# A hybrid graph-attention and Mamba network on one core: x of the first batch loaded first and in pieces, its group norm ahead of the mixer's weights, decay rates and taps broadcast by their loads

## The chip, the core and the metric

The kernel runs on one core of a Trainium2 chip, as a single launch. The core has five engines that each work through a queue of their own: TensorE (PE in the profile; its weight loads are listed apart, as PEld), VectorE (DVE), ScalarE (ACT), GpSimd (POOL) and SyncE (SP), which here only issues DMAs. The metric is the time of one execution on the device in microseconds, and lower is better. Several executions are timed and the median is given.

## What is computed

The network has four layers on x of shape (4 batches, 32 time steps, 128 nodes, 128 features). Only the start of layer 0 bears on this change. Layer 0 adds to x the result of a graph attention over the nodes followed by a Mamba mixer over the time steps, both on a group norm of x. Cut to that:

```python
def _gn(v, G=32, eps=1e-5):                 # per batch, over time, nodes and 4 features of a group
    g = v.reshape(B_, H_, W_, G, C_ // G)
    m = jnp.mean(g, axis=(1, 2, 4), keepdims=True)
    s = jnp.var(g, axis=(1, 2, 4), keepdims=True)
    return ((g - m) / jnp.sqrt(s + eps)).reshape(v.shape)

x = x + _L0_conv_ref(_gn(x), adj, Wq, Wk, Wv, Wo, bo, ...)
# in it: h = layernorm(h + gat(h, adj, Wq, Wk, Wv, Wo, bo)); then, per node, the mixer on h:
xz = xt @ in_proj
xc, z = xz[..., :256], xz[..., 256:]
xconv = conv_b + sum(conv_w[:, kk] * xp[:, kk:kk + T, :] for kk in range(4))   # the taps
xc = silu(xconv)
dbc = xc @ x_proj
dt = softplus(dbc[..., :8] @ dt_w + dt_b)
A = -jnp.exp(A_log)                          # (256, 16) decay rates
dA = jnp.exp(dt[..., None] * A)
h_t = dA_t * h_(t-1) + dt_t * xc_t * B_t     # scan over the 32 steps
y_t = sum over states of h_t * C_t, + Dp * xc, times silu(z), @ out_w + out_b
```

The group norm of a batch needs all 32 time steps of that batch and nothing of the other batches. The decay rates A are the same for every node, and so are the four taps per channel.

## The kernel before

x stays in SBUF for the whole program as the tile X, with nodes on the 128 partitions, then 128 (batch, time) pairs, then 128 features. The program is built in order: `open` makes constants, `load_x` loads X, `layer0` and the three further layers follow.

`load_x` (line 260) issues four DMAs from SyncE's queue, one per batch, each of 4096 rows of 512 bytes. `layer0` (line 266) then loads and prepares weights. `gat_weights` (line 289) loads six tiles of 64 KB and three columns, all from SyncE's queue, and makes `far` (a mask from the adjacency matrix) and `identb`. `mamba_weights` (line 576) loads the mixer's weights and prepares two large tables that hold the same values on all 128 partitions, because in the mixer the nodes are on the partitions and the channels along the row:

- Ar, 128 x 16 x 256, the decay rates. A_log comes as a small tile with channels on partitions; ScalarE takes its exponential, VectorE negates it, TensorE transposes it, and sixteen matmuls with a column of the identity spread one row each over the partitions, each followed by a copy out of PSUM (lines 607 to 625).
- Wm, 128 x 4 x 256, in_proj times the taps. The taps are transposed with A_log, spread by four matmuls, and multiplied in by VectorE (lines 626 to 633).

After this comes the group norm of batch 0, `gat_head` (line 311): in eight groups of four time steps TensorE transposes x into one of two PSUM banks called pm (line 257), ScalarE copies it to S (line 329) and VectorE takes statistics (line 334). Then these are aggregated (line 344), summed over the four features of a group by two tiny matmuls with g4, and eight VectorE instructions normalize S in place (line 374). The attention `gat` (line 378) begins with matmuls of S with Wq and Wk and their copies out of PSUM by ScalarE (lines 405 and 408). Its buffers lie in the pool l0g, opened after the head.

The mixer `mamba` (line 644) runs once per batch. Its `decay` multiplies dt by Ar on GpSimd (line 675), and `expo` takes the exponential on ScalarE (line 681); there are 496 of each. The group norm of batches 1 to 3 is placed at the end of the mixer of the batch before it (line 848).

The order of work around the change is set in two ways. Instructions of one engine run in the order in which they stand in its queue. The order inside `gat_head`, `gat` and `mamba` is written by a small planner, `Parts`, from costs and dependences given by hand, and pinned by `in_order` (line 227). Outside of these, the tile framework orders instructions itself; so `identb` and `I2` stand ahead of `far` in VectorE's queue. The framework also gives every DMA one of eight completion semaphores in turn; a DMA whose semaphore was used by an earlier one waits on its queue until the earlier one has landed.

Of the kernel before, what the change touches and what calls it, by code (L numbers as in the profile page):

```python
# [12 lines left out]
F32 = mybir.dt.float32  # L13
BF16 = mybir.dt.bfloat16
AF = mybir.ActivationFunctionType
ALU = mybir.AluOpType
# [3 lines left out]
P = 128  # L20
B, T, N, F = 4, 32, 128, 128
# [166 lines left out]
class Kernel:  # L188
# [68 lines left out]
            self.nc.tensor.transpose(pt[:, i, :], s, self.ident[:k, :k])  # L257


    def load_x(self):  # L260
        for b in range(B):
            self.nc.sync.dma_start(
                self.X[:, b * T : (b + 1) * T, :], self.ins["x"][b].rearrange("t n f -> n t f")
            )

    def layer0(self):

        with self.pool("l0h", 1) as hp, self.pool("l0c", 1) as c:
            h1 = hp.tile([P, 3 + T, N], F32, tag="h1", name="h1")
            self.nc.gpsimd.memset(h1[:, :3, :], 0.0)  # L270
            with self.pool("l0k", 1) as k, self.pool("l0kp", 2, True) as pk:
                gw, mw = self.gat_weights(c), self.mamba_weights(c, k, pk)


            with self.pool("l0s", 1) as m, self.pool("l0w", 2) as w, self.pool("l0pm", 2, True) as pm:
                S = m.tile([P, T * N], F32, tag="S", name="S")
                plan = Parts()
                self.gat_head(plan, 0, S, gw, m, pm)
                with self.in_order():
                    plan.emit()  # L280
                for b in range(B):
                    with self.pool("l0g", 2) as g, self.pool("l0sc", 1, True) as ps, self.pool("l0po", 1, True) as po:
                        with self.pool("l0px", 1, True) as px:
                            blk = self.gat(h1, S, gw, mw, g, m, w, ps, po, px, pm)
                    with self.pool("l0m", 1) as y, self.pool("l0m2", 2) as v:
                        with self.pool("l0pa", 2, True) as pa, self.pool("l0y", 1, True) as py:
                            self.mamba(b, h1, S, blk, gw, mw, m, w, y, v, pa, py, pm)

    def gat_weights(self, c):
        nc, ins = self.nc, self.ins  # L290
        Wq, Wk, Wv, Wo = (self.load(c, n, ins[f"L0_conv_{n}"], [P, P]) for n in ("Wq", "Wk", "Wv", "Wo"))
        g4 = self.load(c, "g4", ins["g4"], [P, P])

        adj = self.load(c, "adj", ins["L0_conv_adj"], [P, P])
        far = c.tile([P, P], BF16, tag="far", name="far")
        nc.vector.tensor_scalar(far, adj, 0.0, 1e30, ALU.is_equal, ALU.mult)
        identb = c.tile([P, P], BF16, tag="identb", name="identb")
        nc.vector.tensor_copy(identb, self.ident)
        bo = self.col(c, "bo", ins["L0_conv_bo"])
        nsg = self.col(c, "nsg", ins["L0_conv_ns_g"])  # L300
        nsb = self.col(c, "nsb", ins["L0_conv_ns_b"])
        return Wq, Wk, Wv, Wo, g4, far, identb, bo, nsg, nsb
# [270 lines left out]
            plan.emit()  # L573
        return blk

    def mamba_weights(self, c, k, pk):
# [19 lines left out]
        for j in range(2):  # L596
            nc.vector.tensor_scalar(DD[:, j, :], ident, Dp[:, j : j + 1], None, ALU.mult)
        I2 = c.tile([P, 64], F32, tag="I2", name="I2")
        nc.vector.tensor_tensor(I2, ident[:, :64], ident[:, 64:], ALU.add)
        ob4 = c.tile([1, 4, P], F32, tag="ob4", name="ob4")  # L600
        for i in range(4):
            nc.sync.dma_start(ob4[:, i, :], ins["L0_conv_out_b"].rearrange("(o n) -> o n", o=1))
        ntg = self.row(c, "ntg", ins["L0_conv_nt_g"])
        ntb = self.row(c, "ntb", ins["L0_conv_nt_b"])

        cw = self.load(k, "cw", ins["L0_conv_conv_w"].rearrange("(c p) k -> p c k", p=P), [P, 2, 4])
        A = self.load(k, "A", ins["L0_conv_A_log"].rearrange("(c p) s -> p c s", p=P), [P, 2, 16])
        nc.scalar.activation(A, A, AF.Exp)
        nc.vector.tensor_scalar(A, A, -1.0, None, ALU.mult)
        rows = k.tile([16, 2, 2, P], F32, tag="rows", name="rows")  # L610
        for j in range(2):
            p = pk.tile([P, 2, P], F32, tag="pk", name="pk")
            nc.tensor.transpose(p[:16, 0, :], A[:, j, :], ident)
            nc.tensor.transpose(p[:4, 1, :], cw[:, j, :], ident)
            nc.vector.tensor_copy(rows[:, 0, j, :], p[:16, 0, :])
            nc.vector.tensor_copy(rows[:4, 1, j, :], p[:4, 1, :])

        Ar = c.tile([P, 16, 256], F32, tag="Ar", name="Ar")
        for s in range(16):
            p = pk.tile([P, 256], F32, tag="pr", name="pr")  # L620
            nc.tensor.matmul(
                p, ident[:16, s : s + 1].to_broadcast([16, P]),
                rows[:, 0].rearrange("p j d -> p (j d)"), start=True, stop=True,
            )
            nc.scalar.copy(Ar[:, s, :], p)
        Wm = c.tile([P, 4, 256], F32, tag="Wm", name="Wm")
        for m in range(4):
            p = pk.tile([P, 256], F32, tag="pr", name="pr")
            nc.tensor.matmul(
                p, ident[:4, 3 - m : 4 - m].to_broadcast([4, P]),  # L630
                rows[:4, 1].rearrange("p j d -> p (j d)"), start=True, stop=True,
            )
            nc.vector.tensor_tensor(Wm[:, m, :], inp[:, :256], p, ALU.mult)
        return inp, xp, dtw, ow, cb, DD, I2, ob4, ntg, ntb, Ar, Wm
# [9 lines left out]
    def mamba(self, b, h1, S, blk, gw, mw, m0, w0, m, w, pa, py, pm):  # L644
# [15 lines left out]
        hF, S = S, S.rearrange("p (s d) -> p s d", s=16)  # L660
# [4 lines left out]
        def step(t, g, before):  # L665

            k, i = divmod(t, 4)
            cs, h, v, parts = slice(i * P, i * P + P), g["h"], {}, {}
# [9 lines left out]

            def expo(q):
                v["a", q] = pa.tile([P, 4, 256], F32, tag="pa", name="pa")  # L680
                nc.scalar.activation(v["a", q], v.pop(("e", q)), AF.Exp)  # L681

            def diag(q):
                v["D", q] = w.tile([P, 4, 64], F32, tag="D", name="D", bufs=4)
# [2227 lines left out]
```

## Time and profile before

| | us |
|---|---|
| three runs | 4092.22, 4085.39, 4095.92 |
| their median | 4092.22 |
| the profiled execution | 4087.14 |
| its span, first to last instruction | 4085.3 |
| its mean granted TensorE clock | 0.891 of full speed |

Where the span goes by stage, read from the busy time of the engines in stretches (layer 0 ends near 2386 us, when the first loads of layer 1 are issued):

| stretch, us | PE busy | DVE busy | ACT busy | POOL busy | granted clock |
|---|---|---|---|---|---|
| 0 to 102 | 50.67 | 31.32 | 26.67 | 10.18 | 0.95 |
| 350 to 600 (attention, then mixer) | 213.25 | 237.47 | 220.88 | 232.21 | 0.91 |
| 2390 to 2990 (layer 1) | 461.84 | 398.19 | 257.58 | 180.37 | 0.76 |
| 3520 to 4086 (layer 3) | 446.50 | 286.09 | 332.79 | 200.97 | 0.88 |

Busy time is the time in which an engine executed something. In the mixer VectorE and GpSimd are busy over 90% of the time. The first hundred microseconds are different from all the others: no engine is busy for much over half of them.

The last lines of SyncE's queue in this stretch are issues of 0.4 us each, one after the other: for instance bo at 29.05, Dp at 33.63, ntg at 35.38 and cw at 36.26. VectorE's first DD product, which needs Dp, starts at 35.82.

### The profile page before, as it was taken

The page shows a single profiled execution, that of the slowest core. Times are in us where ns is not written, and L with a number is a line of the kernel's source. Part 1 is how long each engine was busy: PE and PEld are TensorE (multiplying, and loading weights), DVE is VectorE, ACT ScalarE, POOL GpSimd, SP SyncE. Part 2 cuts the span into 40 slices and gives each one's busy share as a digit, 9 for nine tenths or more (in the row PEclk, how much of TensorE's full clock was granted, in tenths as well). Part 3 has the DMA queues.
Part 4 walks back from the last instruction along what each step waited for, and adds up shares of the span by engine and source line. Part 5 has one row for each costly group of instructions (what it writes and reads, how often), then busy time and mean ns, then how long its engine had stood idle before and what let it go on. Part 6 is the DMA issues. An engine that isn't in the chain of part 4 may idle for free. (4 is left out here: it accounts for less than half of the span.)

```text
span 4085.3 us, 64261 instructions
## 1 busy us (share of the span) xinstructions
PE 3284.1 (80%) x23384; PEld 2080.5 (51%) x23384; DVE 3077.7 (75%) x7597; ACT 2647.8 (65%) x5230; POOL 2332.0 (57%) x1691
## 2 busy tenths in 40 slices
PE   4888887888887888878888878887747878888777
PEld 2444544445544445444444556654436634466545
DVE  3889997799997799987899964678758763545842
ACT  2699884699875799856898833345545562366753
POOL 0399993599873799963899830424444431114840
PEclk9999899999888899988999776888779999798989
DMA  2000000000000000000000000000020005100002
GB/s 93 1 1 1 1 1 1 1 1 1 1 1 1 1 1 1 1 1 1 1 1 1 1 18 1 1 1 1 1 91 1 1 1 191 64 1 1 1 0 83
DMA packets 48684, 58.74 MB, mean 14 GB/s; under 512 B 6207, under 2 KB 27404, under 8 KB 48364
## 3 DMA queue, kind: packets, MB, share of 16 engines
q1 hardware_dynamic: 34636, 39.91, 2.9%
q10 hardware_dynamic: 13728, 14.68, 1.0%
q8 instruction: 187, 3.06, 0.3%
q14 instruction: 133, 1.09, 0.1%
HBM read 46.19 MB, written 8.39 MB: 13 GB/s over the span
## 5 line engine op out<-in xcount | busy, mean ns | idle before, releaser
L675 POOL TENSOR_TENSOR e<-dt,Ar 128x1024 f32<-128x1024 f32 x496 | 1161.9, 2366 | 102.4 <-ACT pa L681 100.2
L703 DVE SCALAR_TENSOR_TENSOR S<-u,BC,pa 128x256 f32<-128x256 f32 x1984 | 820.8, 476 | 28.4 <-PE yp L718 0.5
L695 DVE TENSOR_TENSOR pa<-pa,S 128x1024 f32<-128x1024 f32 x496 | 607.4, 1225 | 51.7 <-ACT pa L681 51.4
L681 ACT ACTIVATE pa<-e 128x1024 f32<-128x1024 f32 x496 | 504.7, 1022 | 123.6 <-DVE S L703 107.9
L718 PE MATMUL yp<-S,D 64*64 64x256 f32 x4096 | 380.1, 415 | 100.8 <-DVE S L703 84.2
L718 PE MATMUL yp<-S,Dp 64*64 64x256 f32 x4096 | 341.2, 449 | 51.0 <-DVE S L703 40.2
L718 PEld LDWEIGHTS yp<-S,D 64*64 64x64 f32 x4096 | 186.2, 140 | 265.3 <-DVE S L703 156.6
L718 PEld LDWEIGHTS yp<-S,Dp 64*64 64x64 f32 x4096 | 174.8, 152 | 204.0 <-issue 120.5
L459 POOL TENSOR_TENSOR e<-e,den 128x512 f32<-128x512 f32 x128 | 132.4, 1045 | 242.3 <-DVE den L455 180.7
L687 ACT ACTIVATE D<-I,BC 128x64 f32<-128x64 f32 x1024 | 260.8, 334 | 0.6 <-PE yp L718 0.6
L897 PE MATMUL pm<-h,Wm 128*128 128x512 f32 x512 | 242.5, 609 | 1.2 <-ACT h L519 1.2
L736 PE MATMUL pm<-I,y 128*128 128x64 f32 x1024 | 164.6, 288 | 92.6 <-ACT y L726 92.6
L447 ACT ACTIVATE e<-sc,mn 128x128 f32<-128x128 f32 x512 | 143.9, 391 | 94.9 <-DVE mn L442 93.5
L736 PEld LDWEIGHTS pm<-I,y 128*128 128x128 f32 x1024 | 151.7, 213 | 104.8 <-ACT y L726 104.8
L681 ACT ACT_TABLE_LOAD x144 | 184.8, 1283 | 20.4 <-DVE S L703 18.2
L692 POOL TENSOR_TENSOR Dp<-I,BC 128x256 f32<-128x256 f32 x256 | 162.5, 652 | 22.0 <-PE pm L257 11.6
L251 POOL TENSOR_TENSOR rs<-rs,mhalf 128x4 f32<-128x4 f32 (+1 forms) x33 | 38.7, 1173 | 220.5 <-DVE rs L250 179.4
L442 DVE TENSOR_REDUCE mn<-sc 128x4 f32<-128x512 f32 x128 | 83.4, 686 | 81.7 <-PE sc L434 50.0
L897 PEld LDWEIGHTS pm<-h,Wm 128*128 128x128 f32 x512 | 92.2, 194 | 93.1 <-issue 91.0
L2592 ACT ACTIVATE xn<-X,xnb,xrs 128x128 f32<-128x128 f32 x256 | 105.5, 483 | 49.4 <-DVE xnb L2589 49.0
L731 PE MATMUL pm<-xc,DD 128*128 128x128 f32 x512 | 127.1, 333 | 8.0 <-ACT sz L867 7.3
L731 PEld LDWEIGHTS pm<-xc,DD 128*128 128x128 f32 x512 | 86.9, 208 | 67.1 <-issue 38.1
(593 smaller groups left out, 8023.5 us busy)
## 6 DMA issues: line engine op xcount, KB each, us to landing
w<-in_L_ffn_weight_dram SPq DMA_DIRECT2D x22, 1024.0 KB
w<-in_L_ffn_weight_dram ACTq DMA_DIRECT2D x10, 1024.0 KB
out_dram<-o ACTq DMA_DIRECT2D x16, 256.0 KB
out_dram<-o SPq DMA_DIRECT2D x16, 256.0 KB
sh<-in_sh_dram SPq DMA_DIRECT2D x1, 512.0 KB
inp<-in_L_conv_in_proj_dram SPq DMA_DIRECT2D x1, 256.0 KB
rep<-in_rep_dram SPq DMA_DIRECT2D x1, 256.0 KB
raw<-in_L_attn_w_in_dram SPq DMA_DIRECT2D x3, 64.0 KB
```

The costliest lines, as they stand in the source:

```text
L447: nc.scalar.activation(e[:, i, :], v["sc"][:, h, i * P : (i + 1) * P], AF.Exp, scale=-1.0, bias=v["mn"][:, 4 * h + i : 4 * h + i + 1],)
L459: nc.gpsimd.tensor_tensor(v["e", h], v["e", h], den, ALU.mult)
L675: nc.gpsimd.tensor_tensor(v["e", q], node("dt").unsqueeze(1).to_broadcast([P, 4, 256]), Ar[:, 4 * q : 4 * q + 4, :], ALU.mult)
L681: nc.scalar.activation(v["a", q], v.pop(("e", q)), AF.Exp)
L687: nc.scalar.activation(v["D", q][:, r, :], I2, AF.Copy, scale=g["BC"][:, i, s : s + 1])
L692: nc.gpsimd.tensor_tensor(v["D", q], I2.unsqueeze(1).to_broadcast([P, 4, 64]), C, ALU.mult)
L695: nc.vector.tensor_tensor(v["a", q], v["a", q], S[:, 4 * q : 4 * q + 4, :], ALU.mult)
L703: nc.vector.scalar_tensor_tensor(S[:, s, :], node("u"), Bt, a[:, r, :], ALU.mult, ALU.add)
L718: nc.tensor.matmul(v["y"][o : o + 64, n, :256], D[ns, r, :], S[ns, s, :], start=(s < 2), stop=(s >= 14), skip_group_check=True,)
L731: nc.tensor.matmul(v["p"][:, j * P : (j + 1) * P], DD[:, j, :], g["xc"][:, j, cs], start=True, stop=False)
L736: nc.tensor.matmul(v["p"][:, o : o + 64], v["y"][:, n, j * P : (j + 1) * P], I2, start=False, stop=(n == 1))
L897: nc.tensor.matmul(g["x", j], Wm[:, i, j * P : (j + 1) * P], rows(4 * k + 3 - i), start=(i == 0), stop=(i == 3))
```

## The change

There are five edits, all in layer 0's preparation.

1. `load_x` takes a batch and a range of time steps. Batch 0 is loaded in four pieces of eight time steps at the head of `layer0`; batches 1 to 3 are loaded after the mixer's weights.
2. The six 64 KB loads of `gat_weights` are issued from ScalarE's queue, g4 first.
3. `mamba_weights` only issues loads and returns a function `built` with the arithmetic; the group norm of batch 0 is emitted before `built()` is called.
4. A_log and the taps are loaded with their broadcast to 128 partitions: A is now 128 x 256 x 16 (16 KB per partition) and cw 128 x 256 x 4 (4 KB per partition). One ScalarE activation takes the exponential of A, reads it with the states outermost, and writes Ar; VectorE multiplies in_proj with cw directly. The transposes, the broadcasting matmuls, their copies and the PSUM pool l0kp are gone.
5. Ar holds the positive exponential; the sign moves into `expo` as scale=-1.0.

```diff
-    def load_x(self):
-        for b in range(B):
-            self.nc.sync.dma_start(
-                self.X[:, b * T : (b + 1) * T, :], self.ins["x"][b].rearrange("t n f -> n t f")
-            )
+    def load_x(self, b, t0=0, t1=T):
+        self.nc.sync.dma_start(
+            self.X[:, b * T + t0 : b * T + t1, :], self.ins["x"][b, t0:t1].rearrange("t n f -> n t f")
+        )
...
-            with self.pool("l0k", 1) as k, self.pool("l0kp", 2, True) as pk:
-                gw, mw = self.gat_weights(c), self.mamba_weights(c, k, pk)
...
-                plan = Parts()
-                self.gat_head(plan, 0, S, gw, m, pm)
-                with self.in_order():
-                    plan.emit()
+
+                for t in range(0, T, 8):
+                    self.load_x(0, t, t + 8)
+                gw = self.gat_weights(c)
+                with self.pool("l0k", 1) as k:
+                    mw, built = self.mamba_weights(c, k)
+                    for b in range(1, B):
+                        self.load_x(b)
+                    plan = Parts()
+                    self.gat_head(plan, 0, S, gw, m, pm)
+                    with self.in_order():
+                        plan.emit()
+                    built()
...
-        Wq, Wk, Wv, Wo = (self.load(c, n, ins[f"L0_conv_{n}"], [P, P]) for n in ("Wq", "Wk", "Wv", "Wo"))
-        g4 = self.load(c, "g4", ins["g4"], [P, P])
-
-        adj = self.load(c, "adj", ins["L0_conv_adj"], [P, P])
+        g4 = self.load(c, "g4", ins["g4"], [P, P], nc.scalar)
+        Wq, Wk, Wv, Wo = (self.load(c, n, ins[f"L0_conv_{n}"], [P, P], nc.scalar) for n in ("Wq", "Wk", "Wv", "Wo"))
+
+        adj = self.load(c, "adj", ins["L0_conv_adj"], [P, P], nc.scalar)
...
-        cw = self.load(k, "cw", ins["L0_conv_conv_w"].rearrange("(c p) k -> p c k", p=P), [P, 2, 4])
-        A = self.load(k, "A", ins["L0_conv_A_log"].rearrange("(c p) s -> p c s", p=P), [P, 2, 16])
-        nc.scalar.activation(A, A, AF.Exp)
-        nc.vector.tensor_scalar(A, A, -1.0, None, ALU.mult)
...
+        A = self.load(k, "A", ins["L0_conv_A_log"].rearrange("(o d) s -> o d s", o=1).to_broadcast([P, 256, 16]), [P, 256, 16])
+        cw = self.load(
+            k, "cw", ins["L0_conv_conv_w"].rearrange("(o d) k -> o d k", o=1).to_broadcast([P, 256, 4]), [P, 256, 4]
+        )
         Ar = c.tile([P, 16, 256], F32, tag="Ar", name="Ar")
...
         Wm = c.tile([P, 4, 256], F32, tag="Wm", name="Wm")
...
+        def built():
+            for j in range(2):
+                nc.vector.tensor_scalar(DD[:, j, :], ident, Dp[:, j : j + 1], None, ALU.mult)
+            nc.vector.tensor_tensor(I2, ident[:, :64], ident[:, 64:], ALU.add)
+
+            nc.scalar.activation(Ar, A.rearrange("p d s -> p s d"), AF.Exp)
+
+            for m in range(4):
+                nc.vector.tensor_tensor(Wm[:, m, :], inp[:, :256], cw[:, :, 3 - m], ALU.mult)
+
+        return (inp, xp, dtw, ow, cb, DD, I2, ob4, ntg, ntb, Ar, Wm), built
...
-                nc.scalar.activation(v["a", q], v.pop(("e", q)), AF.Exp)
+                nc.scalar.activation(v["a", q], v.pop(("e", q)), AF.Exp, scale=-1.0)
```

In the queues of the changed program VectorE has far, identb, I2, the eight statistics, the first DD product, the aggregate, the second DD product, the rest of the group norm, the eight normalizations, the four Wm products, and then the attention's first reduction. ScalarE has the six issues, the table load, the eight copies of the group norm, the exponential of A, and then the attention's first copy of q, whose buffer lies where A and cw lay.

More of the change, by code (lines that the diff above doesn't have):

```diff
@@ L574, in gat, with mamba_weights @@
         return blk
-    def mamba_weights(self, c, k, pk):
+    def mamba_weights(self, c, k):
         nc, ins, ident = self.nc, self.ins, self.ident
@@ L595, in mamba_weights @@
         DD = c.tile([P, 2, P], F32, tag="DD", name="DD")
-        for j in range(2):
-            nc.vector.tensor_scalar(DD[:, j, :], ident, Dp[:, j : j + 1], None, ALU.mult)
         I2 = c.tile([P, 64], F32, tag="I2", name="I2")
-        nc.vector.tensor_tensor(I2, ident[:, :64], ident[:, 64:], ALU.add)
         ob4 = c.tile([1, 4, P], F32, tag="ob4", name="ob4")
@@ L604, in mamba_weights @@
         ntb = self.row(c, "ntb", ins["L0_conv_nt_b"])
-        cw = self.load(k, "cw", ins["L0_conv_conv_w"].rearrange("(c p) k -> p c k", p=P), [P, 2, 4])
-        A = self.load(k, "A", ins["L0_conv_A_log"].rearrange("(c p) s -> p c s", p=P), [P, 2, 16])
-        nc.scalar.activation(A, A, AF.Exp)
-        nc.vector.tensor_scalar(A, A, -1.0, None, ALU.mult)
[L610 to L616, printed above, removed]
@@ L618, in mamba_weights @@
-        Ar = c.tile([P, 16, 256], F32, tag="Ar", name="Ar")
[L619 to L625, printed above, removed]
-        Wm = c.tile([P, 4, 256], F32, tag="Wm", name="Wm")
[L627 to L633, printed above, removed]
@@ L634, in mamba_weights @@
-        return inp, xp, dtw, ow, cb, DD, I2, ob4, ntg, ntb, Ar, Wm
+        A = self.load(k, "A", ins["L0_conv_A_log"].rearrange("(o d) s -> o d s", o=1).to_broadcast([P, 256, 16]), [P, 256, 16])
+        cw = self.load(
+            k, "cw", ins["L0_conv_conv_w"].rearrange("(o d) k -> o d k", o=1).to_broadcast([P, 256, 4]), [P, 256, 4]
+        )
+        Ar = c.tile([P, 16, 256], F32, tag="Ar", name="Ar")
+        Wm = c.tile([P, 4, 256], F32, tag="Wm", name="Wm")
+        def built():
[5 more added lines that the diff above has]
+                nc.vector.tensor_tensor(Wm[:, m, :], inp[:, :256], cw[:, :, 3 - m], ALU.mult)
@@ L2903 @@
             k.open(c, c)
-            k.load_x()
             k.layer0()
```

## The prediction

> **What bounds the kernel now.** I read the page first, then the stretches of the first 60 us, then the timeline there. The page's totals name no single engine, and the chain of waits covers only the last 35 us (the output stores), so neither says anything about the start of the program, which is all that the change rewrites.
>
> ```profile
> span 4085.3 us, 64261 instructions
> PE 3284.1 (80%) x23384; PEld 2080.5 (51%) x23384; DVE 3077.7 (75%) x7597; ACT 2647.8 (65%) x5230; POOL 2332.0 (57%) x1691
> DMA out_dram<-o 1%; DVE o L2887 0%; PE po L257 0%; DVEq L2887 0%
> ```
>
> The start has to be read from the busy time by stretch (columns: stretch, its length, busy us of each engine with the number of instructions, granted clock, DMA share, GB/s):
>
> ```profile
> 0.00:5.00 5.00, 0.00 (x0) 0.00 (x0) 0.62 (x2) 1.28 (x1) 1.42 (x12) 1.00 0.39 105
> 10.00:15.00 5.00, 0.00 (x0) 0.00 (x0) 0.00 (x0) 0.00 (x0) 0.00 (x0) 1.00 1.04 361
> 25.00:30.00 5.00, 0.00 (x0) 0.00 (x0) 0.00 (x0) 0.00 (x0) 0.00 (x0) 1.00 0.73 245
> 35.00:40.00 5.00, 0.00 (x0) 0.00 (x0) 0.57 (x3) 0.23 (x1) 0.00 (x0) 1.00 0.21 31
> ```
>
> For 40 us the engines do 4.4 us of work between them (0.23 of it in the stretch left out from 30 to 35), while the DMAs first carry all four batches of x (8.4 MB at some 360 GB/s, to about 27 us), then two dozen small loads. The timeline names the order (start, length, engine, line, what, and in brackets the idle time before and its releaser):
>
> ```profile
> 1.35 18.82 SPq L262 DMA_DIRECT2D X<-in_x_dram  x4
> 20.23 6.40 SPq L200 DMA_DIRECT2D Wq<-in_L_conv_Wq_dram  x1
> 36.73 0.47 SPq L200 DMA_DIRECT2D A<-in_L_conv_A_log_dram  x1
> 39.65 0.23 ACT L608 ACTIVATE A<-A 128x32 f32<-128x32 f32 x1 [37.63 <-DMA A<-in_L_conv_A_log_dram]
> 41.62 14.02 PE L621 MATMUL pr<-rows,ident 16*128 16x256 f32 x32 [0.37 <-DVE rows L615]
> 59.11 0.42 DVE L633 TENSOR_TENSOR Wm<-inp,pr 128x256 f32<-128x256 f32 x1 [0.43 <-PE pr L629]
> 59.58 1.57 PEld L257 LDWEIGHTS pm<-ident,X 128*128 128x128 f32 x8 [1.23 <-DVE Wm L633]
> 67.18 0.37 DVE L344 BATCH_NORM_AGGREGATE gmv<-gst 128x2 f32<-128x48 f32 x1
> 70.30 3.74 DVE L374 TENSOR_SCALAR S<-S,gd 128x512 f32<-128x512 f32 x8 [0.82 <-POOL gd L362]
> 73.02 0.60 ACT L408 ACTIVATE q<-pm 128x512 f32<-128x512 f32 x1 [6.66 <-PE pm L405]
> ```
>
> It is one serial chain: x of all batches, small loads, A_log last (39.65), its broadcast through TensorE (to 56), the taps Wm (to 59.5), and only then the first transpose of x, although x had been there since 27. ScalarE's first copy of q, at 73.02, is my reference point: apart from the lines that the diff touches, the instructions of every engine stand in the same order in both programs. The whole of the rest should therefore move by what this copy moves. I call that the shift.
>
> **What the Trainium skill says.** "ScalarE: Activation LUTs", section on what ACT_TABLE_LOAD costs, gives an ACTIVATE with immediate scale and bias 186 ns + 0.833 ns per element. The trace agrees: 128x1024 in 1022 ns (1039 by the formula). "SBUF — State Buffer", section on the DMA port swizzle, says that an access which leaves its 16-byte line each time pays a penalty; the trace has one such SBUF read, a DVE reduction with a 128-byte step (line 1487), 1006 ns against 686 for a contiguous one of as many elements:
>
> ```profile
> L1487 DVE TENSOR_REDUCE ms<-mh 128x32 f32<-128x512 f32 x1 | 1.0, 1006 | 0.0
> L1464 DVE TENSOR_REDUCE mx<-S 128x16 f32<-128x512 f32 x1 | 0.7, 686 | 0.0
> ```
>
> "DMA: Bandwidth & Descriptors", latency and other measured facts, reports 103 GB/s when 128 rows of 16 KB are read in lock-step at a bad pitch; no row of this trace reads so, and I use it only as the pessimistic end for the broadcast load.
>
> **The change part by part.**
>
> *The chain removed.* x of batch 0 goes first, in four pieces of 512 KB, so its transposes no longer follow A_log's landing, the transposes of A_log and cw, the 16 + 4 broadcast matmuls and the 16 copies (40.2 to 56.0) or Wm.
>
> *x and the group norm.* SP issues fr at 0.73 and piece 1 at 1.35; first data at 3 us as now. By the program's waits the third piece waits for fr, the fourth for Wq (its semaphore was used by it), both landing at about 3 to 4. The six 64 KB loads on ScalarE's queue run on the same DMAs: 2.1 + 0.4 MB at 360 GB/s is 7 us, so the last piece lands near 10. On ScalarE's queue the last of these issues, adj, waits for g4; behind it stand only the table load and the first copy, ready by about 5, no loss. On DVE far waits for adj (about 6), with identb and I2 behind it, before the first statistics: no loss either. Last two groups after 10: transposes 1.3, copy 0.6, statistics 0.7, so 12.7.
>
> *A new wait.* DVE has the first DD product between the last statistics and the aggregate, and it needs Dp. SP reaches Dp after bo, nsg, nsb, inp, xp twice, dtw twice, ow and cb; the two dtw loads wait for pieces 3 and 4 to land (10), then three issues of 0.43 us: Dp is issued at 11.4 to 11.9 and lands 1.7 us after (33.63+0.46 to 35.82 now), 13.6. Aggregate at 14.1. From there 3.1 us to the first norm as now (67.18 to 70.30): 17.2, q's matmul done near 20.
>
> *A_log and taps by broadcast.* A is now 2.1 MB (128 rows of 16 KB, all from the same 16 KB), cw 0.5 MB. Issue: four ob4 (1.20), ntg, ntb after Dp: 14.1; data from about 16. Rate: x's 370 GB/s gives 5.7 us. The nearest broadcasts in the trace, ntg and ntb at 37 to 38 us, ran at 81 GB/s with the DMAs half busy (share 0.50, second number from the end below), so about 160 when busy: 13 us. The skill's 103 gives 20 us. I take 300, near x's rate, because rows of 16 KB are long where ntg's have 512 bytes and mix with 4-byte loads: 7 us, and 0.7 to the semaphore. A lands at 23.7, cw 1.7 later at 25.4.
>
> ```profile
> 37.50:38.00 0.50, 0.00 (x0) 0.00 (x0) 0.00 (x0) 0.00 (x0) 0.00 (x0) 1.00 0.50 81
> ```
>
> *The exponential.* One ACTIVATE over 4096 elements, read with a 64-byte step. Without a penalty 0.19 + 4096 x 0.833 = 3.6 us; with the trace's strided price (320 ns on 512, 0.63 ns each) 6.2. I take 6.2: 23.7 to 29.9. It stands on ScalarE ahead of the first q copy, so everything waits here. Four Wm products on DVE (0.42 each now, 0.7 with the same penalty) end by 28, and also gate q, whose buffer reuses A's and cw's space; they are hidden by the exponential.
>
> *Sum.* q's copy starts at 30 instead of 73.0: shift 43. Behind it k's copy can follow at once (its matmul is long done), where now it waited until 74.72; of that 1.1 us I count 0.8. Together 44 us.
>
> *Edits at nothing.* scale=-1.0 in the 496 decay exponentials: immediate scale; L2075 with it takes 630 ns for 128x512, L2706 without it 632. DD, I2 lie in DVE's waits. x of batches 1 to 3 (6.3 MB, 17 us) is issued behind cw and lands near 43; batch 1 is first read by its group norm hundreds of us later, so it is hidden; if it delayed A it would be counted above, but it is queued behind it.
>
> **Rivals.**
> 1. *The broadcast is slow.* All engines read one 16 KB stretch. For it: ntg's half rate. Against: rows 32 times as long. At 160 GB/s A lands 29.7, the exponential ends 36; at 103, with 2 us less sure each way, A lands 37, exp ends 43 (cw lands 42, Wm 45): shift 37 to 28, time about 4053 to 4062.
> 2. *The rest doesn't follow the shift.* PE's granted clock is 0.76 to 0.98 by stage and may fall otherwise; the runs shown differ by 10 us among themselves. Nothing in the order of the instructions speaks for a systematic share; 4035 to 4055 around the forecast.
> 3. *Quick all through.* x's rate for A and no stride penalty: A at 22.4, exp ends 26, shift 47 + 0.8: about 4042, as far below as the scatter then allows, 4035.
> 4. *Slower than before.* The broadcast loads are cut into one descriptor per 64-byte row of A, 32768 of them. x's 4096 descriptors take 5.6 us, so 45 us: A lands at 61.7, exp ends 68, then cw's 32768 in 16-byte pieces land at 107 and Wm ends at 110: q's copy 37 us later than now, about 4127. It decides from the point where exp or Wm ends after 73, that is if A takes over 50 us or both loads over 53. Against it: the program lists A as 128 x 4096 and cw as 128 x 1024, merged rows.
>
> **How the numbers follow.** The profiled execution took 4087.14 us, 1.8 more than its span; the runs shown have median 4092.22. With the shift of 44 these give 4043 and 4048; I forecast 4045, between them. Chances: forecast, with rival 2 as its scatter, 0.74; slow broadcast 0.14; quick 0.07; a broadcast so slow that nothing is gained 0.02; slower 0.03. The forecast's own range is 4036 to 4055; taking in most of the slow broadcast, 4035 to 4062. A difference under 0.3% (12 us) could not be told from none here. Faster 0.95, same 0.02, slower 0.03.
>
> **What would show it.** Right: first transposes of x near 6 us; aggregate near 14 with idle time before DD put to Dp; the exponential of A as one ACTIVATE of about 6 us starting near 24 after a DMA wait; q's copy near 30; layer 1's first loads at 2386.5 - 44. Wrong: A landing after 30 (rate), an exponential of 3.6 (penalty), the shift at q's copy not kept at 2386, or hundreds of short packets for A.

## The result and the profile after

The changed kernel takes 4047.52 us (median of four runs, 4034.41 to 4049.71), the kernel before in the same comparison 4094.07 (4085.39 to 4097.13); the ratio is 0.9883, interval 0.9857 to 0.9909. The forecast was 4045, in the range 4035 to 4062. The profiled execution took 4047.38 us. The two medians lie 46.6 us apart; the interval of the ratio allows 37 to 59.

The page of the changed kernel, span and totals by engine:

```profile
span 4045.5 us, 64158 instructions
PE 3273.5 (81%) x23340; PEld 2076.8 (51%) x23340; DVE 3074.7 (76%) x7592; ACT 2648.3 (65%) x5214; POOL 2333.1 (58%) x1691
```

No engine lost more than 11 us of busy time (TensorE, 3284.1 to 3273.5), while the span fell by 39.8: what went is idle time at the start. The same four stretches as before (stretch, length, busy us of PE, PEld, DVE, ACT and POOL with counts, granted clock, DMA share, GB/s):

```profile
0.00:5.00 5.00, 0.00 (x0) 0.00 (x0) 0.00 (x0) 1.12 (x1) 1.41 (x12) 1.00 0.53 148
10.00:15.00 5.00, 2.67 (x15) 1.99 (x15) 4.61 (x10) 2.36 (x5) 0.00 (x0) 0.99 0.45 103
25.00:30.00 5.00, 0.00 (x0) 0.00 (x0) 2.21 (x4) 5.00 (x1) 0.00 (x0) 0.51 0.99 351
35.00:40.00 5.00, 5.00 (x47) 2.78 (x46) 1.29 (x2) 1.35 (x5) 0.00 (x0) 0.96 1.03 374
```

From 10 to 15 us, where nothing computed before, the group norm's statistics now run. From 25 to 30 there is still only one ScalarE instruction and the tap products. The DMAs now stay busy past 40 us (share 1.03 from 35 to 40, before 0.21), but what they carry after the taps have landed at 25.8 is x of the batches 1 to 3, for which nobody waits in this stretch. The timeline (start, length, engine, line, what; in brackets the idle time before and its releaser):

```profile
5.71 7.11 PE L257 MATMUL pm<-ident,X 128*128 128x128 f32 x32 [5.71 <-DMA X<-in_x_dram]
14.35 0.29 DVE L618 TENSOR_SCALAR DD<-ident,Dp 128x128 f32<-128x128 f32 x1 [0.18 <-DMA Dp<-in_L_conv_Dp_dram]
14.55 0.37 DVE L350 BATCH_NORM_AGGREGATE gmv<-gst 128x2 f32<-128x48 f32 x1
14.84 0.43 SPq L200 DMA_DIRECT2D A<-in_L_conv_A_log_dram  x1
18.00 3.74 DVE L380 TENSOR_SCALAR S<-S,gd 128x512 f32<-128x512 f32 x8 [0.75 <-POOL gd L368]
...
24.51 7.12 ACT L621 ACTIVATE Ar<-A 128x4096 f32<-128x4096 f32 x1 [11.07 <-DMA A<-in_L_conv_A_log_dram]
25.80 2.21 DVE L624 TENSOR_TENSOR Wm<-inp,cw 128x256 f32<-128x256 f32 x4 [4.05 <-DMA cw<-in_L_conv_conv_w_dram]
31.66 0.60 ACT L414 ACTIVATE q<-pm 128x512 f32<-128x512 f32 x1
32.16 0.59 ACT L414 ACTIVATE k<-pm 128x512 f32<-128x512 f32 x1
32.31 2.07 PE L411 MATMUL pm<-S,Wq 128*128 128x512 f32 x2 [10.20 <-ACT q L414]
37.88 1.29 DVE L448 TENSOR_REDUCE mn<-sc 128x4 f32<-128x512 f32 x2 [9.88 <-PE sc L440]
```

The chain has become short: A's issue, its landing, the exponential, q's copy. The group norm and q's product stand beside it (TensorE starts that product 0.6 us after the first norm, and then is idle 10.2 us until q's copy). q's copy moved from 73.02 to 31.66, 41.4 us; the first reduction of the scores (before at 79.28, now 37.88) also moved by 41.4. I use this reduction as the mark in the experiments, since it holds what happens to k's copy as well. Its line before:

```profile
79.28 1.29 DVE L442 TENSOR_REDUCE mn<-sc 128x4 f32<-128x512 f32 x2 [5.24 <-PE sc L434]
```

### The profile page after: what moved, and what is told of

Read it like the earlier page. It is cut to its first block, busy times and chain, and to the rows that moved or that the text cites. A ratio compares the mean times of both kernels' runs of the same rounds, so it can differ in the third digit from the quotient of the medians.

```text
span 4045.5 us, 64158 instructions
## 1 busy us (share of the span) xinstructions
PE 3273.5 (81%) x23340; PEld 2076.8 (51%) x23340; DVE 3074.7 (76%) x7592; ACT 2648.3 (65%) x5214; POOL 2333.1 (58%) x1691
## 5 line engine op out<-in xcount | busy, mean ns | idle before, releaser
L673 ACT ACTIVATE pa<-e 128x1024 f32<-128x1024 f32 x496 | 504.9, 1023 | 127.0 <-DVE S L695 114.9
L673 ACT ACT_TABLE_LOAD x144 | 184.8, 1283 | 19.4 <-DVE S L695 17.2
```

Source lines behind the costliest of these rows:

```text
L673: nc.scalar.activation(v["a", q], v.pop(("e", q)), AF.Exp, scale=-1.0)
```

## The experiments

**Is it the order or the broadcast?** Two kernels with one half of the change each. The first has the new order, but loads the decay rates and taps small and spreads them with TensorE as before:

```diff
-        A = self.load(k, "A", ins["L0_conv_A_log"].rearrange("(o d) s -> o d s", o=1).to_broadcast([P, 256, 16]), [P, 256, 16])
...
+        A = self.load(k, "A", ins["L0_conv_A_log"].rearrange("(c p) s -> p c s", p=P), [P, 2, 16])
...
-            nc.scalar.activation(Ar, A.rearrange("p d s -> p s d"), AF.Exp)
+            nc.scalar.activation(A, A, AF.Exp)
...
+            for s in range(16):
...
+                nc.scalar.copy(Ar[:, s, :], p)
```

> The new order of the loads and the group norm ahead of the tables, but A_log and the taps small and spread by TensorE as before. Theory: the order is most of the gain and the broadcast loads add some 10 us. The spreading starts when VectorE is through with the eight normalizations (21.7), takes 18 us, and q's matmul stands behind it on TensorE, so the copy of q comes at 42 (shift 31), time about 4060. Rival: the gain is from the removal of the spreading on TensorE; then the copy of q comes at 60 or later and the time is above 4078.

Timeline of the kernel with the order alone:

```profile
17.68 0.23 ACT L619 ACTIVATE A<-A 128x32 f32<-128x32 f32 x1 [4.58 <-DMA A<-in_L_conv_A_log_dram]
23.55 14.02 PE L629 MATMUL pr<-rows,ident 16*128 16x256 f32 x32 [0.37 <-DVE rows L625]
41.10 0.60 ACT L414 ACTIVATE q<-pm 128x512 f32<-128x512 f32 x1 [3.12 <-PE pr L636]
47.35 1.29 DVE L448 TENSOR_REDUCE mn<-sc 128x4 f32<-128x512 f32 x2 [5.88 <-PE sc L440]
```

The second keeps the order of before and only takes the broadcast loads, the one exponential and the scale of -1:

```diff
+        A = self.load(k, "A", ins["L0_conv_A_log"].rearrange("(o d) s -> o d s", o=1).to_broadcast([P, 256, 16]), [P, 256, 16])
...
+        nc.scalar.activation(Ar, A.rearrange("p d s -> p s d"), AF.Exp)
...
-                nc.scalar.activation(v["a", q], v.pop(("e", q)), AF.Exp)
+                nc.scalar.activation(v["a", q], v.pop(("e", q)), AF.Exp, scale=-1.0)
```

> The old order (all of x first, tables before the group norm) with A and the taps broadcast by their loads and one exponential of A. Theory: A is issued near 36.5, lands near 46, its exponential of 7.1 us stands ahead of the group norm's copies on ScalarE and ends at 53; copy of q near 64, shift 9, time about 4084. Rival (the broadcast is the gain): copy of q before 50, time below 4070.

Its timeline:

```profile
44.14 7.13 ACT L611 ACTIVATE Ar<-A 128x4096 f32<-128x4096 f32 x1 [42.13 <-DMA A<-in_L_conv_A_log_dram]
51.30 1.07 ACT L329 COPY S<-pm 128x512 f32<-128x512 f32 x2
64.58 0.60 ACT L408 ACTIVATE q<-pm 128x512 f32<-128x512 f32 x1 [6.91 <-PE pm L405]
70.23 1.29 DVE L442 TENSOR_REDUCE mn<-sc 128x4 f32<-128x512 f32 x2 [4.63 <-PE sc L434]
```

The order alone brings the first reduction from 79.28 to 47.35, 31.9 us; the broadcast alone to 70.23, 9.05 us. The sum is 41.0, the whole change has 41.4. The times agree: the order alone 4058.85, ratio 0.9929 (0.9908 to 0.9949); the broadcast alone 4084.2, ratio 0.9975 (0.9963 to 0.9988). So about three quarters of the gain come from the order, one quarter from the way of spreading. A second profile of the kernel before (below) has its first reduction at 77.62; counted from there the order alone brings 30.3 us, the broadcast alone 7.4, the whole change 39.7, so each of these figures is uncertain by 1 to 2 us.

The small load lands at 17.68, 6.8 us ahead of the large one, and loses that and 9.4 us more. Part of this is a wait: TensorE transposes A_log at 22.12 only, behind the first products with Wq and Wk, which wait for the norm. Then come the spreading and the taps, to 41.0. The forecast of 42 for q's copy was met by another path than the expected one: q's product stands ahead of the spreading in TensorE's queue (at 18.55), not behind it, and what releases the copy by the trace is the last product of the taps.

**Which order: that of the loads or that of the instructions?** All loads stand as in the changed kernel, but the built parts (diagonal products, exponential, tap products) go back ahead of the group norm:

```diff
                     with self.in_order():
+                        built()
                         plan.emit()
-                    built()
```

> The changed kernel with all its loads where they are, but the built parts (diagonal products, exponential, tap products) issued ahead of the first batch's copies, statistics and norm on ScalarE and VectorE, as in the kernel before. It tells how much of the gain is the order of the instructions and not that of the loads. My theory: the in-order engines make the whole group norm wait for the exponential, which ends at 31.6 as in the changed kernel; from there the eight copies, the norm and q's product take the 13.3 us that they took in the run with the broadcast loads alone (exponential over at 51.27, q's copy at 64.58), so q's copy comes at about 45 instead of 31.66, and the first reduction of the scores at about 50.6 instead of 37.88: 13 us lost, about 4061. The rival: the order of the loads is what counts and the engines catch up, as the transposes can run ahead on TensorE: q's copy before 36 and a loss below 5 us, 4053 or less.

Its timeline:

```profile
24.38 7.12 ACT L621 ACTIVATE Ar<-A 128x4096 f32<-128x4096 f32 x1 [19.21 <-DMA A<-in_L_conv_A_log_dram]
31.40 1.05 ACT L335 COPY S<-pm 128x512 f32<-128x512 f32 x2
38.50 0.37 DVE L350 BATCH_NORM_AGGREGATE gmv<-gst 128x2 f32<-128x48 f32 x1
44.51 0.60 ACT L414 ACTIVATE q<-pm 128x512 f32<-128x512 f32 x1 [6.77 <-PE pm L411]
49.97 1.29 DVE L448 TENSOR_REDUCE mn<-sc 128x4 f32<-128x512 f32 x2 [4.49 <-PE sc L440]
```

x had been in SBUF since 11 us or so, but ScalarE's first copy of its transposes stands behind an exponential that waits for a load until 24.38. q's copy comes at 44.51, 12.9 us later than in the changed kernel, the first reduction at 49.97, 12.1 later, as I expected. The median of five runs is 4064.21 (ratio 0.9910, 0.9878 to 0.9942), some 16 above the changed kernel. Putting the group norm ahead is thus worth some 12 us. The kernel with the broadcast alone has these instructions in the same order as this one, and the old order of the loads, and its first reduction came at 70.23: 20.3 us later. So with the broadcast in place, the order of the loads is worth some 20 us and that of the instructions some 12. Without the broadcast the two were not parted. Of the loads' 20 us only the pieces were tried by themselves (below), not the six loads moved to ScalarE's queue.

**What makes the exponential last 7.12 us?** The forecast had 6.2 for a read with a 64-byte step. My first theory put it all on the reads:

```diff
-            nc.scalar.activation(Ar, A.rearrange("p d s -> p s d"), AF.Exp)
+            nc.scalar.activation(Ar.rearrange("p s d -> p d s"), A, AF.Exp)
```

> One line of the changed kernel differs: the exponential of the decay rates reads its 4096 elements of a partition in the order in which they lie, and writes its result with a step of 1024 bytes (the changed kernel reads with a step of 64 bytes and writes in order). My theory is that the step of the reads makes the exponential last 7.12 us instead of the 3.6 us that 4096 elements take at the 0.83 ns of an element of other ScalarE rows. It expects 3.6 us here, the exponential over by 28.1, the first copy of q then at about 28.2 instead of 31.7 (the copies' inputs have been ready since 20.6), and some 3.5 us off the time, about 4044 beside a changed kernel at 4048. The rival: a step costs the same on either side. Then the exponential still takes about 7 us (or more, as the step is now 16 times larger) and nothing moves: q at 31.7 or later, 4048 or more.

That theory fell: read in order and written with a step of 1024 bytes, the exponential took 7.23 us (24.29 to 31.52), q's copy came at 31.55, and the median was 4053.61 (4050.53 to 4058.08), no gain. It remained open whether steps cost on both sides or whether 4096 exponentials simply take 7 us, so I timed the instruction by itself: nine such instructions (rows) over the same tiles, put ahead of the kernel's own exponential, which overwrites them (four of them here):

```diff
+            nc.scalar.activation(Wf, Af, AF.Exp)
...
+            nc.scalar.activation(Wf.rearrange("p (s a) -> p s a", s=4), Af.rearrange("p (a s) -> p s a", s=4), AF.Exp)
...
+            nc.scalar.activation(Wf.rearrange("p (a s) -> p s a", s=4), Af.rearrange("p (s a) -> p s a", s=4), AF.Exp)
...
+            nc.vector.tensor_copy(Wf.rearrange("p (s a) -> p s a", s=4), Af.rearrange("p (a s) -> p s a", s=4))
```

> Durations alone count here. To the kernel with the rates' load first, nine rows over the same 128 x 4096 floats are added ahead of its own exponential, which overwrites what they write: on ScalarE the exponential in order on both sides, a plain copy in order, the exponential with reads at a step of 16 and of 32 bytes, and with writes at a step of 16 and of 64 bytes; on VectorE copies in order and with reads at a step of 16 and of 64 bytes. Theory A, after the run with the step on the write side gave 7.23 us: a step on either side costs ScalarE about twice, so in order on both sides takes 3.4 to 3.6 us (4096 at 0.83 ns, and 0.2), the copy the same, and the stepped ones 7 us each, or less at 16 bytes. Theory B: the step has no part in it, and an exponential of 4096 elements just out of this load takes 7 us in any order, so that the row in order on both sides takes 7 too, and the copy 3.6 if it is the function, 7 if it is the tile. The whole should be some 45 us longer than without these rows.

The instructions that write Ar, by line (ns min/median/max, start, shape). In this order: ScalarE's exponential in order (L623), its copy in order (L624), the exponential with reads at 16 and at 32 bytes (L625, L626), with writes at 16 and at 64 bytes (L627, L628); VectorE's copy in order (L629), with reads at 16 and at 64 bytes (L630, L631):

```profile
L623 ACT ACTIVATE Ar<-A x1: 3619/3619/3619, 15.7 to 15.7; 128x4096 f32<-128x4096 f32 x1
L624 ACT ACTIVATE Ar<-A x1: 3617/3617/3617, 19.4 to 19.4; 128x4096 f32<-128x4096 f32 x1
L625 ACT ACTIVATE Ar<-A x1: 7452/7452/7452, 23.0 to 23.0; 128x4096 f32<-128x4096 f32 x1
L626 ACT ACTIVATE Ar<-A x1: 7559/7559/7559, 30.5 to 30.5; 128x4096 f32<-128x4096 f32 x1
L627 ACT ACTIVATE Ar<-A x1: 7433/7433/7433, 38.1 to 38.1; 128x4096 f32<-128x4096 f32 x1
L628 ACT ACTIVATE Ar<-A x1: 7066/7066/7066, 45.6 to 45.6; 128x4096 f32<-128x4096 f32 x1
L629 DVE COPY Ar<-A x1: 2294/2294/2294, 52.7 to 52.7; 128x4096 f32<-128x4096 f32 x1
L630 DVE COPY Ar<-A x1: 3823/3823/3823, 55.0 to 55.0; 128x4096 f32<-128x4096 f32 x1
L631 DVE COPY Ar<-A x1: 3617/3617/3617, 58.8 to 58.8; 128x4096 f32<-128x4096 f32 x1
```

In order, ScalarE needs 3.62 us for the exponential and for the copy; with a step on either side, from 16 bytes on (less was not tried), 7.1 to 7.6 us. So it is the step that doubles the row, on the write side as on the read side, and an instruction that swaps channels and states has a step on one of the two. Traffic of the DMAs is not the reason: the last of ScalarE's stepped rows still took 7.07 us, with the DMAs idle from 46 us on. VectorE pays 1.3 to 1.5 us for reads at 16 and 64 bytes. The unstepped price is that of the Trainium skill, "ScalarE: Activation LUTs", section on what ACT_TABLE_LOAD costs: 186 + 4096 x 0.833 = 3598 ns, against 3619. The rows were added to the kernel with the early load that is shown further down. They push its q's copy from 23.67 to 69.72, by 46 us, and the one execution took 4083.84, 43.4 above that kernel's median of 4040.41: a microsecond ahead of q's copy is close to a microsecond of the whole.

**What are the pieces of x worth?** One load of 2 MB instead of four of 512 KB:

```diff
-                for t in range(0, T, 8):
-                    self.load_x(0, t, t + 8)
+                self.load_x(0)
```

> The changed kernel with x of the first batch fetched by one transfer of 2 MB instead of four of 512 KB; the order is kept. My theory is that the pieces bring the first transposes, the statistics and the norm forward, but that the end of the stage is set by the load of the decay rates and the exponential behind it, which this edit touches only through SP's queue: three issues less on it, some 1.4 us, while the diagonal products stand behind the same aggregate. It expects the first transpose at about 13 instead of 5.7, the aggregate at 17.5 to 18.5 instead of 14.55, the normed tiles some 3 to 4 us later, and q's first copy at 31 to 33 (31.66 in the changed kernel): the time the same within 2 us. The rival is that the pieces are part of the gain: q's copy 3 to 4 us later, at 35 or more, and 4052.

Its timeline:

```profile
17.12 0.42 SPq L200 DMA_DIRECT2D A<-in_L_conv_A_log_dram  x1
19.85 0.37 DVE L349 BATCH_NORM_AGGREGATE gmv<-gst 128x2 f32<-128x48 f32 x1
26.70 7.13 ACT L620 ACTIVATE Ar<-A 128x4096 f32<-128x4096 f32 x1 [7.69 <-DMA A<-in_L_conv_A_log_dram]
33.87 0.60 ACT L413 ACTIVATE q<-pm 128x512 f32<-128x512 f32 x1
```

The aggregate comes 5.3 us later (19.85 against 14.55, later than I expected), and that does not matter, for q's copy still follows the exponential directly. But q's copy is 2.2 us later, between theory and rival, and by a path that I had the wrong way round: with fewer issues A's load goes out later, at 17.12 instead of 14.84, because SP's queue has waits in it (the issue of bo stays open from 2.93 to 8.26, and inp is issued at 11.42 only, when x has landed: the first transposes start at 11.54). The pieces are worth 2.2 us, through the queue behind them, and none through the norm. In the time (4053.46, 4043.78 to 4059.39) 2 us cannot be seen.

**If A's landing sets the end, A should be loaded first.** The loads of the rates and taps directly behind x's pieces, the built parts behind the norms:

```diff
                 for t in range(0, T, 8):
                     self.load_x(0, t, t + 8)
...
+                    A = self.load(k, "A", ins["L0_conv_A_log"].rearrange("(o d) s -> o d s", o=1).to_broadcast([P, 256, 16]), [P, 256, 16])
...
+                    gw = self.gat_weights(c)
+                    mw, built = self.mamba_weights(c, k, A, cw)
...
                     with self.in_order():
                         plan.emit()
-                    built()
+                        built()
```

> The changed kernel with the loads of the decay rates and of the taps issued on SP directly behind x's four pieces, ahead of the graph block's and the mixer's other weights, and with the built parts (the diagonal products, the exponential, the tap products) put behind the norms on VectorE. Nothing else moves. My theory is that the exponential waits for its load alone, that the load waits for its place in SP's queue, and that q's copy stands behind the exponential: the load issued at about 6.5 instead of 14.84 lands at 16.5 to 18.5 instead of 24.51 (the same bytes at the same 300 GB/s, behind x's pieces), the exponential of 7.1 us ends at 24 to 25.6, and q's first copy comes at about 25 instead of 31.66: 6 to 7 us off the time, about 4041. The rival is that the load's bytes, once ahead, hold up x's pieces or the weights of the norm and the projections (they share the transfer rate), so that the statistics and q's product move back: the first norm at 22 or later, q's copy at 29 or later, and a gain below 3 us.

Its timeline:

```profile
5.82 1.81 SPq L200 DMA_DIRECT2D A<-in_L_conv_A_log_dram  x1
13.95 0.37 DVE L355 BATCH_NORM_AGGREGATE gmv<-gst 128x2 f32<-128x48 f32 x1
15.76 7.28 ACT L622 ACTIVATE Ar<-A 128x4096 f32<-128x4096 f32 x1 [3.01 <-DMA A<-in_L_conv_A_log_dram]
17.10 3.74 DVE L385 TENSOR_SCALAR S<-S,gd 128x512 f32<-128x512 f32 x8 [0.75 <-POOL gd L373]
21.29 2.21 DVE L625 TENSOR_TENSOR Wm<-inp,cw 128x256 f32<-128x256 f32 x4
23.67 0.60 ACT L419 ACTIVATE q<-pm 128x512 f32<-128x512 f32 x1 [0.63 <-DVE Wm L625]
30.92 1.29 DVE L453 TENSOR_REDUCE mn<-sc 128x4 f32<-128x512 f32 x2 [7.42 <-PE sc L445]
```

A lands at 15.76 and holds nothing up: the aggregate and the norms are even 0.6 and 0.9 us earlier. Some 0.4 us of this is that the first diagonal product, with its wait for Dp, no longer stands ahead of the aggregate. q's copy comes at 23.67, 8.0 us ahead of the changed kernel, the first reduction at 30.92, 7.0 ahead. The bracket shows the next bound: the tap products, on VectorE behind the norms (q's buffer reuses the space of A and cw).

Both edits together, the early load and the exponential read in order:

> The two edits together: the loads of the decay rates and taps directly behind x's pieces, and the exponential reading in order. If both theories hold, the exponential runs from about 17.5 to 21 and q's first copy is then released by its own product (20.6 in the changed kernel, where the norm sets it) or by the exponential, whichever is later: at about 21 to 22, some 10 us before the 31.66 of the changed kernel, and 4038. If the step costs writes as much as reads, it is no better than the edit of the order alone, about 4041; if the early load delays the norm, q's product and with it q's copy come at 25 or later.

It could not do better after what reading in order had shown: the exponential took 7.36 us, q's copy came at 23.56, and the median was 4044.7 (4039.93 to 4054.78, ratio 0.9887, 0.9866 to 0.9907), within the scatter of the early load's 4040.41.

**The scatter.** The changed kernel and the early load were run again, and the kernel before once:

> The changed kernel once more, unchanged, for a second profile and more rounds. In the first profile ScalarE's first copy of q came 41.4 us earlier than before, the first load of layer 1 44.2 us earlier, the middle of layer 1 47.9, its end only 37.6, the last instruction 39.8. Theory: what happens to the shift after the copy of q is scatter of the granted TensorE clock; then the copy of q stays at 31.7 within 0.3 us, and the length from there to the end differs from the first profile's by several us, above all in layer 1. Rival: the 10 us lost in layer 1 are a consequence of the change; then the stage is as long as in the first profile, within 1 us. Time: 4035 to 4050.

> The kernel before once more, for a second profile. Theory: copy of q at 73.0 within 0.3 us, and the length of layer 1 (first load to the first load of layer 2, 600.3 us in the first profile) differs by several us without any change of the program. Rival: 600 within 1 us.

> The kernel with the rates' and taps' loads directly behind x's pieces, once more, on the same chip as the changed kernel that follows. If the 7.0 us by which its first reduction of the scores came earlier (30.92 against 37.88) reach the end, its median lies 5 to 9 us under that of the changed kernel; the rival is that the scatter of one program from run to run (4040 to 4055 for the changed kernel so far) hides it, and the medians lie within 3 us or the other way round.

> The changed kernel beside it: about 4048, q's first copy at 31.7 and the first reduction at 37.9, as in its two profiles so far.

The changed kernel gave 4048.26 (ratio 0.9903, 0.9883 to 0.9923) and 4049.73 (0.9905, 0.9880 to 0.9930), its first reduction at 37.90 and 38.46. The early load gave 4041.43 (ratio 0.9864, 0.9834 to 0.9894) after 4040.41 (0.9881, 0.9853 to 0.9910). On the same chip as the changed kernel it was 8.3 us below it, as its trace says (first reduction at 30.29), with intervals that still overlap. It is the best version that I have: its first reduction is earlier in both profiles, while in the time the gain is likely but not clear of the scatter.

The second profile of the kernel before has a span of 4100.3, 15 us above the first, for the same program. Its start missed my expectation: q's copy came at 71.39 and not within 0.3 us of 73.0, as A_log had landed at 38.03 instead of 39.65. So the shift by the change is 39.7 or 41.4 us, by which profile of before one takes. The changed kernel's start repeated (31.70 and 31.26).

A stage of layer 1 shows where part of the 15 us comes from. From the start of its first to the start of its last instruction of line 1694 it took 281.3 us in the first profile and 290.0 in the second, and 290.0 in the changed kernel too. The windows that begin 160 us into this stage, for before (first profile), before again, and the changed kernel:

```profile
2835.00:2875.00 40.00, 32.78 (x200) 20.57 (x203) 32.06 (x115) 25.23 (x57) 18.75 (x30) 0.87 0.01 1
```

```profile
2838.00:2878.00 40.00, 37.95 (x195) 25.23 (x195) 26.76 (x95) 18.56 (x39) 13.71 (x21) 0.70 0.00 1
```

```profile
2789.00:2829.00 40.00, 37.95 (x193) 25.18 (x193) 26.73 (x96) 18.56 (x39) 13.62 (x22) 0.70 0.01 1
```

The granted clock (the third number from the end) was 0.87 in one profile and 0.70 in the others, with TensorE busy 33 of 40 us or 38. At the lower clock VectorE and ScalarE were busy for 26.7 and 18.6 of the 40 us, instead of 32.1 and 25.2. The program alone does not decide it: before had it both ways. But my theory that the changed kernel's layer 1 would differ from profile to profile fell: all three of its profiles have 607 us from the first load of layer 1 to that of layer 2 and 290.0 in the stage, as the rival had it; before had 600.3 in the first profile and 607.2 in the second. Over all fourteen profiles the stage took 281.3 or 290.0 us, within 0.1. The three short ones began between 2665 and 2675 us, the eleven long ones at 2660 or earlier or at 2678. So it is not excluded that the stage's length hangs on when it is reached, and then that the shift itself costs 7 to 9 us there against the first profile of before.

Likewise the stretch from the first reduction to layer 1's first load took 2301.7 to 2323.3 us over these profiles, which are of ten programs; the early load alone had 2305.4 and 2322.1. What decides the clock in an execution stayed open.

## Why the prediction was right

*The reading of the profile held.* The start was one serial chain with no engine at work, and the rest moved with q's copy, as far as the scatter lets one see. First transposes: forecast "near 6", measured 5.71. Layer 1's first load: forecast 2386.5 - 44, measured 2342.29, which is 2386.53 - 44.24. This last agreement is partly luck: 41.4 came from the start, and 2.8 from the scatter of layer 0 (2307.2 us from the first reduction to that load in one profile, 2304.4 in the other). The end is partly luck too: 4045 was taken between 4043 and 4048, and the shift was put 2.6 us too high, while the medians moved by 5 us more than the start. With 41.4 us the median of before on record, 4092.22, would have given 4050.8.

*The sum, term by term.* The forecast shift was 44: 43 at q's copy and 0.8 for k. Measured were 41.4 at q's copy and nothing more. Three terms make the difference.
- A's landing: forecast 23.7, measured 24.51. Its issue was 0.7 late (14.84 for 14.1); the time from issue to landing, 9.67, was as forecast (9.6). The assumed 300 GB/s held as a mean, which was not known beforehand: the DMAs moved some 210 GB/s for all loads together from 17 to 19 us and 360 to 460 from then to A's landing. The slow broadcast (rival 1) did not occur.
- The exponential: forecast 6.2, measured 7.12. The penalty was taken from a VectorE reduction with a step of 128 bytes, 0.63 ns on an element; ScalarE pays (7.12 - 3.62) / 4096 = 0.85 ns. These two terms, 0.8 and 0.9, are the 1.7 us by which q's copy is later than the forecast 30.
- k's 0.8 us: k's copy does follow at once, at 32.16, as forecast. The next group's products on TensorE also start 0.8 us sooner behind q's copy (0.65 us instead of 1.46), but they then take 3.5 us instead of 2.8, so that from q's copy to the reduction it is 6.22 us after and 6.26 before. The lines are the second of these products in each kernel (before, after):

```profile
76.19 1.06 PE L405 MATMUL pm<-S,Wk 128*128 128x512 f32 x2
34.18 1.61 PE L411 MATMUL pm<-S,Wk 128*128 128x512 f32 x2
```

The granted clock was 0.50 in both kernels when these products began. Before, it was 0.94 from 76 to 78 us, during the second; after, it was 0.66 from 34 to 36. Why it rises when it does stayed open. TensorE's 10.2 us of idleness alone is not the reason: in the kernel with the order alone it had worked until 0.74 us before, and the clock was 0.50 as well.

*Hidden steps.* The last statistics ended at 14.17, not 12.7, so the wait for Dp ahead of the aggregate was 0.18 us instead of 0.9; the aggregate came at 14.55 (forecast 14.1), the first norm at 18.00 (17.2), 3.45 us behind the aggregate and not 3.1. None of it counts, since q's product was ready long before its copy could run. The experiment with x in one piece shows how much cover there was: 5.3 us more on the aggregate cost nothing by themselves. The tap products took 0.61 us each (0.7 was allowed) and ended at 28.0, under the exponential. The scale of -1.0 is free, as forecast: the 496 exponentials take 1023 ns each against 1022.

*The rivals.* "Slower than before" needed descriptors of 64 bytes and A landing after 50 us or more later; A's load took 9.67 us, where the 32768 descriptors of that rival were put at 45. The 103 GB/s that the first rival took from the Trainium skill are given there for copies between two tensors in the chip's memory, with the lock-step as an inference; they say little about this load, and no run here shows that case. "Quick all through" missed because of the step, and because A landed 2.1 us later than it assumed. "The rest doesn't follow" is what is seen in single runs (4034 to 4059 for the changed kernel); whether a share of it, in layer 1, belongs to the change stayed open.

*What was not seen.* That A's landing, once it is the bound, could be had 9 us earlier by SP's queue alone. The forecast had all the numbers for it: it counted what stands ahead of A in the queue, and did not ask whether A has to stand behind it.

## What to carry to other kernels

At the start of a program look for stretches without any engine at work and order loads and instructions by the chain that ends last there; an in-order engine with an early wait for a late load holds back work whose data has long been present (12 us here). A broadcast by the load can beat a spread on TensorE though it moves 128 times the bytes (by 7 to 9 us here in the old order, by 9 in the new), and its place in the queue counts: after the change, the place of that one load was worth another 7 to 8 us at the first reduction. Price a rearranging operand before moving it onto the critical path, and count what waits inside an issuing queue as well as what it issues.

## What the hardware showed that was not expected

- ScalarE over 128 x 4096 floats: 3.62 us in order, 7.07 to 7.56 us with a step of 16 to 64 bytes on reads or writes, 7.23 with writes at 1024 bytes. The penalty is all there at 16 bytes. VectorE's copy: 2.29 us in order, 3.82 with reads at 16 bytes, 3.62 at 64. The Trainium skill, "SBUF — State Buffer", section on the DMA port swizzle, speaks of a penalty when accesses leave a 16-byte line each time; these rows agree with it, for reads on both engines and for writes on ScalarE.
- One stage of the same program took 281.3 or 290.0 us, with a granted clock of 0.87 or 0.70 in 40 us of it, and nothing between over fourteen profiles; single runs of one program lay between 4075 and 4111.
